# One fixed TensorE order for the attention of a transformer block: runs of eight transposes, the projection and the transposes of the residual moved

## The chip, the cores and the metric

The kernel runs on one core of one Trainium2 chip. The metric is device time in microseconds; lower is better. The core has a matrix engine (TensorE; PE in the profile, with PEld for its weight loads), a vector engine (VectorE, DVE), a scalar engine (ScalarE, ACT), GpSimd (POOL), and SyncE (SP), which here only issues DMA transfers. Each engine works through its own queue in order, and semaphores hold an instruction back until what it needs is there. TensorE writes its results into eight banks of PSUM, each 128 partitions by 512 floats; ACT and DVE read them from there.

## The reference

One block of 2048 tokens of width 1024 in float32: a normalised input goes through single-head attention with head width 256, its output is projected, normalised and added to the input, and the same is done with a gated feed-forward network (FFN) of hidden width 2752.

```python
def layernorm(x): return (x - mean(x)) / sqrt(var(x) + 1e-5)

def attention(x):                       # x: (1, 2048, 1024)
    q, k, v = split(x @ Wqkv + bqkv)    # each (2048, 256)
    a = softmax(q @ k.T / 16)           # (2048, 2048)
    return (a @ v) @ Wo + bo            # (2048, 1024)

def ffn(x):
    return (silu(x @ W_gate.T) * (x @ W_up.T)) @ W_down.T   # hidden width 2752

x = x + layernorm(attention(layernorm(x)))
x = x + layernorm(ffn(layernorm(x)))
```

## The kernel before

**Precision.** Almost every product is made of three matmuls of a fast 32-bit type. A matrix is split into a high part (`split`, L109: a cast on ACT) and a low part (L110: the source minus the high part, on DVE). `mm3` (L144 to L148) multiplies high by high, high by low and low by high into one PSUM bank.

**Stages.** From 0 to about 163 us the input is normalised and transposed, and q, k and v are made (`v_block`, L206 to L211, leaves its sum in bank 6 or 7, from which DVE takes it at L210 and L211). From about 163 to 437 us runs the attention with the projection and the first part of the residual. From then to the end the FFN runs as a Strassen-like scheme of products (L605).

**Attention.** The 2048 queries are 16 blocks (`NT`) of 128; the main loop (L898 to L940) goes over them, and in block i the following is called:

- `q_load` (L240), in blocks 4 and 8 (`TB` is 4): SP loads the next 512 queries, and ACT and DVE split them into `qa` or `qb`, the two buffers used in turn.
- `turn(i, j)` for j = 0 to 3 (L263 to L270): four 128x128 transposes of the exponentials `p_s` (L268) into bank 4 or 7, split into `pT` by ACT and DVE.
- `scores(i+1, j)` (L243 to L251): six 512-wide matmuls into bank j, and on DVE the row maximum of the bank (L251).
- `softmax(i+1)` (L253 to L261): DVE takes the maximum of four (L256) and multiplies it by -1/16 (L257); ACT makes four exponentials, each with its row sum (L259); DVE adds the sums and takes the reciprocal (L260, L261).
- a load of the rows of x into `pair[i % 3][1]`, for the residual, in the first 8 blocks (`EARLY`).
- `turn_o(i-1)` (L282 to L286): two transposes of the attention's output into bank 5 (L285), split into `oTs`.
- `attend(i)` (L272 to L280): for each of 16 blocks of keys a 512-wide (L276) and a 256-wide matmul (L277) into bank 6; ACT copies one half of the result (L279) and DVE adds the other (L280).
- `proj(i-1)` (L288 to L297): 12 matmuls with the output weights, six into bank 5 and six into bank 7; after each six DVE scales and adds the bias (L295). The weights `wo_s` share their memory (`wvo`) with the value weights of `v_block`.
- `xpose(i-2)`, in blocks 2 to 9 (L342 to L352): eight transposes (L347) of the normalised rows, four to a bank, into banks 6 and 5; ACT copies each bank out (L349) and SP stores it as FFN input (L351).
- `residual(i-1)`, in blocks 1 to 8 (L299 to L308): statistics on DVE (L116 twice, L119, L120), the power -1/2 on POOL (L121) and the product for the bias (L302), the normalisation on ACT (L303), the sum with x on DVE (L304) and its store (L305), statistics again with POOL (L307), and the second normalisation on ACT (L308), whose result `xpose` reads one block later in the loop.

In blocks 10 to 15 the first loads, sums and splits of the FFN are also called, and `feed` and `order` bring its first weights.

**What sets the order.** The lines above are only the order in which instructions are handed to the scheduler of the tile framework (`schedule_with_timeline_sim=True`). It puts the instructions of every engine into an order of its own, by its own timeline, as long as dependences through tiles and banks hold. `tc.keep_in_program_order` takes an instruction out of its choice: such instructions follow each other in the order of the program. Before, it is used in the FFN (under the name `pin`, L403) and for the late residuals' statistics. A long run of one kind therefore need not stay together: in this trace TensorE's attention is a mixture, such as one attend matmul between four transposes and a score matmul.

Of the kernel before, what the change touches and what calls it, by code (L numbers as in the profile page):

```python
# [11 lines left out]
ALU = mybir.AluOpType  # L12
# [3 lines left out]
P = 128  # L16
T = 2048
C = 1024
D = 256
F = 2752  # L20
NT = T // P
# [3 lines left out]
TB = G // P  # L25
FB = F // P
FR = F - FB * P
NKB = T // P
# [6 lines left out]
def block_kernel(ctx, tc, x, wqk, wv, bqk, bv, wo, bo, wgu, wlast, wd, out):  # L35
# [12 lines left out]
    nc = tc.nc  # L48
# [4 lines left out]
    def tl(p, shape, dt, name):  # L53
        return p.tile(shape, dt, tag=name, name=name, bufs=1)
# [3 lines left out]
    ident = tl(cpool, [P, P], F32, "ident")  # L58
# [18 lines left out]
    bank = [tl(bank_pool, [P, 512], F32, f"bank{i}") for i in range(8)]  # L77
# [27 lines left out]
    def f32(ap):  # L105
        return ap.bitcast(F32)

    def split(hi, lo, src, lo_engine=None):
        nc.scalar.copy(hi, src)  # L109
        (lo_engine or nc.vector).tensor_tensor(lo, src, f32(hi), ALU.subtract)  # L110
# [30 lines left out]
            cols = slice(tb * P, (tb + 1) * P)  # L141
            split(dst[:, 4 * hf : 4 * hf + 4, 0, cols], dst[:, 4 * hf : 4 * hf + 4, 1, cols], src)

    def mm3(o, w, m, first, last):  # L144

        nc.tensor.matmul(o, w[0], m[0], start=first, stop=False)  # L146
        nc.tensor.matmul(o, w[0], m[1], start=False, stop=False)  # L147
        nc.tensor.matmul(o, w[1], m[0], start=False, stop=last)  # L148


    def kT(d, g):
        return slot(kx, 4 * d + g)

    vt = a1.rearrange("p a b c -> p (a b c)").rearrange("p (k h d) -> p k h d", h=2, d=D)
# [75 lines left out]
    nc.scalar.dma_start(bo_s, bo.partition_broadcast(P))  # L230


    qraw = f4[4].rearrange("p (d q) -> p d q", d=2)
    pair = [(f4[0], f4[1]), (f4[2], f4[3]), (f2p[0], f2p[1])]
    wo_s = wvo.rearrange("p a b c -> p (a b c)").rearrange("p (d h c) -> p d h c", d=2, h=2)
    pT = [a2[:, 4 * i : 4 * i + 4, :, :].rearrange("p a b c -> p (a b c)").rearrange("p (k h q) -> p k h q", h=2, q=P) for i in range(2)]
    o_s = [f2[4][:, 0:D], f2[4][:, D:]]
    EARLY = 2 * TB

    def q_load(g):  # L240
        nc.sync.dma_start(qraw, q_d[g])
        split(qs[g % 2][:, :, 0, :], qs[g % 2][:, :, 1, :], qraw)

    def scores(i, j):

        cols = slice((i % TB) * P, (i % TB + 1) * P)
        q = qs[(i // TB) % 2]
        for d in range(2):
            k = kT(d, j)
            mm3(bank[j], (q[:, d, 0, cols], q[:, d, 1, cols]), (k[:, 0, :], k[:, 1, :]), d == 0, d == 1)  # L250
        nc.vector.tensor_reduce(ys[i % 4][:, j : j + 1], bank[j], AX.X, ALU.max)  # L251

    def softmax(i):  # L253

        s = ys[i % 4]
        nc.vector.tensor_reduce(s[:, 4:5], s[:, 0:4], AX.X, ALU.max)  # L256
        nc.vector.tensor_scalar(s[:, 5:6], s[:, 4:5], -1.0 / 16.0, None, ALU.mult)  # L257
        for j in range(4):
            nc.scalar.activation(p_s[:, j * 512 : j * 512 + 512], bank[j], AF.Exp, bias=s[:, 5:6], scale=1.0 / 16.0, accum_out=s[:, 8 + j : 9 + j])  # L259
        nc.vector.tensor_reduce(s[:, 12:13], s[:, 8:12], AX.X, ALU.add)  # L260
        nc.vector.reciprocal(s[:, 13:14], s[:, 12:13])  # L261

    def turn(i, j):  # L263

        b = bank[(4, 7)[j % 2]]
        for n in range(4):
            k = 4 * j + n
            nc.tensor.transpose(b[:, n * P : (n + 1) * P], p_s[:, k * P : (k + 1) * P], ident)  # L268
        d = pT[i % 2][:, 4 * j : 4 * j + 4, :, :]
        split(d[:, :, 0, :], d[:, :, 1, :], b.rearrange("p (n q) -> p n q", n=4))  # L270

    def attend(i):  # L272
        b = bank[6]
        p = pT[i % 2]
        for k in range(NKB):
            nc.tensor.matmul(b, p[:, k, 0, :], vt[:, k, :, :].rearrange("p h d -> p (h d)"), start=(k == 0), stop=False)  # L276
            nc.tensor.matmul(b[:, D:], p[:, k, 1, :], vt[:, k, 0, :], start=False, stop=(k == NKB - 1))  # L277
        o = o_s[i % 2]
        nc.scalar.copy(o, b[:, :D])  # L279
        nc.vector.tensor_tensor(o, b[:, D:], o, ALU.add)  # L280

    def turn_o(i):  # L282
        b = bank[5][:, 0:D]
        for d in range(2):
            nc.tensor.transpose(b[:, d * P : (d + 1) * P], o_s[i % 2][:, d * P : (d + 1) * P], ident)  # L285
        split(oTs[i % 2][:, :, 0, :], oTs[i % 2][:, :, 1, :], b.rearrange("p (d q) -> p d q", d=2))  # L286

    def proj(i):  # L288
        a = pair[i % 3][0] if i < EARLY else f4[i % 2]
        oT = oTs[i % 2]  # L290
        for h, b in ((1, bank[5]), (0, bank[7])):
            cols = slice(h * 512, h * 512 + 512)
            for d in range(2):
                mm3(b, (oT[:, d, 0, :], oT[:, d, 1, :]), (wo_s[:, d, 0, cols], wo_s[:, d, 1, cols]), d == 0, d == 1)
            nc.vector.scalar_tensor_tensor(a[:, cols], b, ys[i % 4][:, 13:14], bo_s[:, cols], ALU.mult, ALU.add)  # L295
        if i >= EARLY:
            nc.sync.dma_start(at_d[i], a)  # L297
# [26 lines left out]
    p_s = tl(spool, [P, T], F32, "p_s")  # L324
# [6 lines left out]
    for j in range(4):  # L331
        scores(0, j)
# [6 lines left out]
        split(wo_s[:, d, 0, :], wo_s[:, d, 1, :], f4[d])  # L339


    def xpose(t, a, b, banks):  # L342
        for hf in range(2):
            o = banks[hf]
            for j in range(4):
                cb = 4 * hf + j
                nc.tensor.transpose(o[:, j * P : (j + 1) * P], a[:, cb * P : (cb + 1) * P], ident)  # L347
            s = b[:, hf * 512 : hf * 512 + 512]
            nc.scalar.copy(s, o)  # L349
            d = xT_d[t // TB][hf * 512 : hf * 512 + 512, (t % TB) * P : (t % TB + 1) * P]  # L350
            nc.sync.dma_start(d.rearrange("(j p) t -> p j t", p=P), s.rearrange("p (j t) -> p j t", j=4))  # L351
# [28 lines left out]
    L, R = slice(0, 512), slice(512, 1024)  # L380
# [19 lines left out]

    pin = tc.keep_in_program_order  # L403

    def split_later(dst, src):

        pin(nc.scalar.copy(dst[:, :, 0, :], src))
        pin(nc.vector.tensor_tensor(dst[:, :, 1, :], src, f32(dst[:, :, 0, :]), ALU.subtract))

    def first_load(cb, r1, r2):  # L410
        load_xq(r1, 0, cb)
        load_xq(r2, 1, cb)

    def first_sums(cb, r1, r2):
        split_later(by_half(xb)[:, :, cb], two(r1))
        sum_x(r1, r2)
        nc.sync.dma_start(xs_d[cb][0], r1)
        nc.sync.dma_start(xs_d[cb][1], r2)

    class First:  # L420
# [10 lines left out]
        def use(self):  # L431
            split_later(self.dst, two(self.r))
# [43 lines left out]
    class Slot:  # L476
        t = None
# [139 lines left out]
    def add(o, a, b, op=ALU.add):  # L617
        nc.vector.tensor_tensor(o, a, b, op)  # L618
# [122 lines left out]
    def down_weights(p):  # L741

        r1, r2 = f4[0:2]
        pin(nc.vector.tensor_tensor(r2[:, R], r2[:, R], r1[:, R], ALU.subtract))
        add(r1[:, R], r1[:, R], r1[:, L], ALU.subtract)
        add(r1[:, L], r2[:, R], r1[:, L])
        add(r2[:, L], r2[:, L], r1[:, L], ALU.subtract)
        for n, t in (("T1", r1[:, R]), ("T3", r2[:, R]), ("T2", r1[:, L]), ("T4", r2[:, L])):
            nc.sync.dma_start(td[p][n], t)
# [148 lines left out]
    room = [(f4[2], f4[3]), (wr[1], xe)]  # L898
    for i in range(NT):
        more = i + 1 < NT  # L900
        if i % TB == 0 and TB <= i < NT - TB:
            q_load(i // TB + 1)
        turn(i, 0)
        turn(i, 1)
        if more:
            scores(i + 1, 0)
            scores(i + 1, 1)
        turn(i, 2)
        turn(i, 3)
        if more:  # L910
            scores(i + 1, 2)
            scores(i + 1, 3)
            softmax(i + 1)
        if i < EARLY:
            nc.sync.dma_start(pair[i % 3][1], x[i * P : (i + 1) * P, :])
        if i > 0:
            turn_o(i - 1)
        if i == NT - 1:
            for f in order[:4]:
                f.use()  # L920
        attend(i)
        if i > 0:
            proj(i - 1)
        if 2 <= i < EARLY + 2:
            xpose(i - 2, *pair[(i - 2) % 3], (bank[6], bank[5]))
        if 0 < i <= EARLY:
            residual(i - 1, *pair[(i - 1) % 3])
        cb = i - EARLY - 3
        if 0 <= cb < 4:
            first_sums(cb, *room[cb % 2])  # L930
        if 0 <= cb + 1 < 4:
            first_load(cb + 1, *room[(cb + 1) % 2])
        if i == NT - 4:
            feed.pump()
        if i == NT - 2:
            for n in range(2):
                slots.free(flat(a2[:, 2 * n : 2 * n + 2, :, :]))
            feed.pump()
            order = [t2[0], t13[0], t13[1], t13[2], t2[1], t13[3]] + t4
            spare = f4[2], f4[3], wr[1], xe  # L940
            for f, r in zip(order, spare):
                f.load(r)
    turn_o(NT - 1)
    proj(NT - 1)

    last = f4[2], f4[3], wr[1], bo_s
# [103 lines left out]
```

## Time and profile before

| What | Value |
|---|---|
| median of 3 runs | 1701.09 us (1698.03 to 1702.44) |
| the profiled execution's own time | 1700.9 us |
| span of the profile | 1699.1 us, 21099 instructions |
| TensorE clock granted in 40 slices | nine tenths or more in every slice |
| transfers over the span | 271.00 MB, mean 159 GB/s |

The span reaches from the first to the last instruction that the profiler saw; the remaining 1.8 us lie around it. The profile divides the span into 40 slices of 42.5 us. Its digits are tenths of the slice in which the engine was busy, and 9 means 90% or more:

```profile
PE   8999999999899999999999999999999999999997
DVE  8643667667787777776578457866555665455458
ACT  3222445544544444443365444433333333344343
```

Slices 5 to 10 are the attention; in slice 11 the FFN begins, and TensorE's digit falls to 8 there. The costliest groups of instructions are all matmuls of the FFN (columns: line, engine, operation, output and inputs, shape, number; busy us and mean ns of one; idle us of the engine just before them):

```profile
L605 PE MATMUL bank<-a 128*128 128x512 f32 x1164 | 274.2, 389 | 0.0
...
L605 PE MATMUL bank<-xb,a 128*128 128x512 f32 x912 | 212.3, 389 | 0.1
...
L276 PE MATMUL bank<-a,a 128*128 128x512 f32 x256 | 94.6, 403 | 2.8 <-ACT f L349 2.0
```

A group's mean is the length of the record of one instruction; consecutive matmuls overlap, so the records of one engine add up to more than its busy time. The last column of the third line names who ended most of the idle time in front of the attend matmuls.

### The profile page before, as it was taken

How to read it: one execution, taken by the hardware profiler on the slowest of the kernel's cores; microseconds unless marked ns; L12 is line 12 of the kernel's file. 1: busy time of each engine (PE TensorE's matmuls, PEld its weight loads, DVE VectorE, ACT ScalarE, POOL GpSimd, SP SyncE). 2: the span in 40 equal slices, each digit the busy share in tenths (PEclk: the TensorE clock that was granted, in tenths of full speed). 3: DMA queues.
4: the chain of work that ended last, by engine and by line, in shares of the span. 5: the costliest groups of instructions: out<-in, count | busy, mean ns of one | idle time of the engine just before them, and what ended most of it. 6: DMA issues, size and time to landing. Idle time of an engine off the chain costs nothing.

```text
span 1699.1 us, 21099 instructions
## 1 busy us (share of the span) xinstructions
PE 1669.2 (98%) x7764; PEld 1385.5 (82%) x7764; DVE 1100.3 (65%) x1682; ACT 694.8 (41%) x1039; POOL 91.3 (5%) x118
## 2 busy tenths in 40 slices
PE   8999999999899999999999999999999999999997
PEld 6888887888678888888888888788888888888886
DVE  8643667667787777776578457866555665455458
ACT  3222445544544444443365444433333333344343
POOL 1000000000011211110000000100000000000001
PEclk9999999999999999999999999999999999999999
DMA  6221123334676566665367666633332223566654
GB/s 214 81 81 38 38 75 121 101 118 169 218 243 209 200 215 212 217 220 183 122 204 252 215 191 198 210 106 113 130 111 100 93 94 124 209 221 192 195 189 158
DMA packets 131014, 271.00 MB, mean 159 GB/s; under 512 B 13280, under 2 KB 29792, under 8 KB 130912
## 3 DMA queue, kind: packets, MB, share of 16 engines
q1 hardware_dynamic: 128176, 262.72, 46.5%
q10 hardware_dynamic: 2736, 6.95, 1.2%
q8 instruction: 60, 0.98, 0.2%
q14 instruction: 42, 0.34, 0.1%
HBM read 185.73 MB, written 83.89 MB: 159 GB/s over the span
## 4 chain that ended last, share of the span: by engine, by line
PE 92%; DVE 4%; DMA 2%; ACT 1%; issue 1%; POOL 0%; SPq 0%; POOLq 0%; DVEq 0%; ACTq 0%
PE bank L605 69%; PE bank L146 4%; PE bank L147 4%; PE bank L148 4%; PE bank L276 3%; PE bank L277 2%; PE bank L206 2%; PE bank L268 1%; PE bank L207 1%; PE bank L347 1%; PE bank L139 1%; DVE a L110 1%; DVE small L116 0%; DMA f<-xT_d 0%; DVE wvo L110 0%
## 5 line engine op out<-in xcount | busy, mean ns | idle before, releaser
L605 PE MATMUL bank<-a 128*128 128x512 f32 x1164 | 274.2, 389 | 0.0
L605 PEld LDWEIGHTS bank<-a 128*128 128x128 f32 x1164 | 218.5, 188 | 45.3
L605 PE MATMUL bank<-xb,a 128*128 128x512 f32 x912 | 212.3, 389 | 0.1
L605 PEld LDWEIGHTS bank<-xb,a 128*128 128x128 f32 x912 | 171.1, 188 | 36.0 <-ACT xi L621 0.6
L618 DVE TENSOR_TENSOR xi<-bank,xi 128x512 f32<-128x512 f32 (+1 forms) x170 | 114.0, 682 | 115.0 <-PE bank L605 70.1
L110 DVE TENSOR_TENSOR a<-f2p,a 128x1024 fp32r<-128x1024 f32 (+2 forms) x133 | 134.6, 1012 | 58.0 <-ACT a L109 54.0
L109 ACT CAST a<-f2p 128x1024 fp32r<-128x1024 f32 (+2 forms) x133 | 117.5, 884 | 131.7 <-PE bank L605 107.2
L110 DVE TENSOR_TENSOR a<-f,a 128x1024 fp32r<-128x1024 f32 (+2 forms) x91 | 89.9, 988 | 106.5 <-ACT a L109 99.8
L605 PE MATMUL bank<-wvo 128*128 128x512 f32 x612 | 149.6, 389 | 0.0
L605 PE MATMUL bank<-kx,a 128*128 128x512 f32 x612 | 146.2, 389 | 0.0
L605 PE MATMUL bank<-a,a 128*128 128x512 f32 x588 | 140.2, 390 | 3.8 <-ACT xi L661 2.6
L605 PEld LDWEIGHTS bank<-kx,a 128*128 128x128 f32 x612 | 114.9, 188 | 23.8
L605 PEld LDWEIGHTS bank<-wvo 128*128 128x128 f32 x612 | 114.9, 188 | 23.9
L605 PEld LDWEIGHTS bank<-a,a 128*128 128x128 f32 x588 | 110.2, 188 | 27.5 <-ACT xi L661 3.0
L109 ACT CAST a<-f 128x1024 fp32r<-128x1024 f32 (+2 forms) x91 | 69.5, 764 | 141.6 <-PE bank L605 110.3
L605 PE MATMUL bank<-a,wvo 128*128 128x512 f32 x444 | 106.3, 389 | 0.0
L605 PE MATMUL bank<-kx,wvo 128*128 128x512 f32 x420 | 100.1, 389 | 0.0
L605 PEld LDWEIGHTS bank<-a,wvo 128*128 128x128 f32 x444 | 83.3, 188 | 17.3
L276 PE MATMUL bank<-a,a 128*128 128x512 f32 x256 | 94.6, 403 | 2.8 <-ACT f L349 2.0
L110 DVE TENSOR_TENSOR wvo<-f,wvo 128x1024 fp32r<-128x1024 f32 (+1 forms) x52 | 60.8, 1169 | 54.9 <-ACT wvo L109 53.8
L605 PEld LDWEIGHTS bank<-kx,wvo 128*128 128x128 f32 x420 | 78.8, 188 | 16.4
L618 DVE TENSOR_TENSOR xi<-xi,xi 128x512 f32<-128x512 f32 (+1 forms) x124 | 85.3, 688 | 5.6 <-ACT xi L621 1.5
(233 smaller groups left out, 2677.5 us busy)
## 6 DMA issues: line engine op xcount, KB each, us to landing
f2p<-wgu SPq DMA_DIRECT2D x41, 512.0 KB, 5.6
hd_S<-xi SPq DMA_DIRECT2D x80, 256.0 KB, 4.4
f<-x SPq DMA_DIRECT2D x30, 512.0 KB, 3.8
hd_A<-xi SPq DMA_DIRECT2D x60, 256.0 KB, 2.0
f<-wgu SPq DMA_DIRECT2D x22, 512.0 KB, 3.5
wr<-wgu SPq DMA_DIRECT2D x21, 512.0 KB, 5.9
f<-wd SPq DMA_DIRECT2D x20, 512.0 KB, 5.0
td_T<-f SPq DMA_DIRECT2D x40, 256.0 KB, 4.6
```

The lines of the kernel that those rows point to most:

```text
L109: nc.scalar.copy(hi, src)
L110: (lo_engine or nc.vector).tensor_tensor(lo, src, f32(hi), ALU.subtract)
L139: nc.tensor.transpose(b[:, j * P : (j + 1) * P], t[:, cb * P : (cb + 1) * P], ident)
L146: nc.tensor.matmul(o, w[0], m[0], start=first, stop=False)
L147: nc.tensor.matmul(o, w[0], m[1], start=False, stop=False)
L148: nc.tensor.matmul(o, w[1], m[0], start=False, stop=last)
L206: nc.tensor.matmul(b, xg[:, c, 0, cols], wv_s[:, c, :, :].rearrange("p a f -> p (a f)"), start=(c == 0), stop=False)
L207: nc.tensor.matmul(b[:, D:], xg[:, c, 1, cols], wv_s[:, c, 0, :], start=False, stop=(c == 7))
L276: nc.tensor.matmul(b, p[:, k, 0, :], vt[:, k, :, :].rearrange("p h d -> p (h d)"), start=(k == 0), stop=False)
L277: nc.tensor.matmul(b[:, D:], p[:, k, 1, :], vt[:, k, 0, :], start=False, stop=(k == NKB - 1))
L605: one = nc.tensor.matmul(o, w[i], m[j], start=first and n == 0, stop=last and n == 2, skip_group_check=chained)
L618: nc.vector.tensor_tensor(o, a, b, op)
```

## The change

It does four things.

1. A new `pin` hands every TensorE instruction of the attention to `keep_in_program_order` in blocks 0 to 12 (`ORDERED` is `NT - 3`, and `block[0]` holds the block that the loop is in). It covers `scores` (not those of block 0 in front of the loop), `turn`, `attend`, `turn_o`, `proj` and, through an argument, `xpose`. The matmuls of the last three blocks stay with the scheduler. The name `pin` of the FFN becomes `keep`.
2. In the program's order, `turn_o(i-1)` stands directly behind `turn(i, 2)` and `turn(i, 3)`, and `xpose(i-2)` directly behind `attend(i)`, ahead of `proj(i-1)`.
3. The banks: the second half of `proj` goes to bank 6, where it went to bank 7; `xpose` goes to banks 4 and 7, where it went to 6 and 5.
4. `q_load` is called in blocks 5 and 9 behind the softmax, where it was called at the start of blocks 4 and 8.

Lines behind the new helper lie further down in the changed kernel: L303 becomes L311, L308 becomes L316, L347 becomes L355.

```diff
--- before.py
+++ after.py
@@ -141,11 +141,11 @@
             cols = slice(tb * P, (tb + 1) * P)
             split(dst[:, 4 * hf : 4 * hf + 4, 0, cols], dst[:, 4 * hf : 4 * hf + 4, 1, cols], src)
 
-    def mm3(o, w, m, first, last):
-
-        nc.tensor.matmul(o, w[0], m[0], start=first, stop=False)
-        nc.tensor.matmul(o, w[0], m[1], start=False, stop=False)
-        nc.tensor.matmul(o, w[1], m[0], start=False, stop=last)
+    def mm3(o, w, m, first, last, pin=lambda i: i):
+
+        pin(nc.tensor.matmul(o, w[0], m[0], start=first, stop=False))
+        pin(nc.tensor.matmul(o, w[0], m[1], start=False, stop=False))
+        pin(nc.tensor.matmul(o, w[1], m[0], start=False, stop=last))
 
 
     def kT(d, g):
@@ -230,6 +230,14 @@
     nc.scalar.dma_start(bo_s, bo.partition_broadcast(P))
 
 
+
+    ORDERED = NT - 3
+    block = [0]
+
+    def pin(i):
+        return tc.keep_in_program_order(i) if block[0] < ORDERED else i
+
+    free = lambda i: i
     qraw = f4[4].rearrange("p (d q) -> p d q", d=2)
     pair = [(f4[0], f4[1]), (f4[2], f4[3]), (f2p[0], f2p[1])]
     wo_s = wvo.rearrange("p a b c -> p (a b c)").rearrange("p (d h c) -> p d h c", d=2, h=2)
@@ -247,7 +255,7 @@
         q = qs[(i // TB) % 2]
         for d in range(2):
             k = kT(d, j)
-            mm3(bank[j], (q[:, d, 0, cols], q[:, d, 1, cols]), (k[:, 0, :], k[:, 1, :]), d == 0, d == 1)
+            mm3(bank[j], (q[:, d, 0, cols], q[:, d, 1, cols]), (k[:, 0, :], k[:, 1, :]), d == 0, d == 1, pin if i else free)
         nc.vector.tensor_reduce(ys[i % 4][:, j : j + 1], bank[j], AX.X, ALU.max)
 
     def softmax(i):
@@ -265,7 +273,7 @@
         b = bank[(4, 7)[j % 2]]
         for n in range(4):
             k = 4 * j + n
-            nc.tensor.transpose(b[:, n * P : (n + 1) * P], p_s[:, k * P : (k + 1) * P], ident)
+            pin(nc.tensor.transpose(b[:, n * P : (n + 1) * P], p_s[:, k * P : (k + 1) * P], ident))
         d = pT[i % 2][:, 4 * j : 4 * j + 4, :, :]
         split(d[:, :, 0, :], d[:, :, 1, :], b.rearrange("p (n q) -> p n q", n=4))
 
@@ -273,8 +281,8 @@
         b = bank[6]
         p = pT[i % 2]
         for k in range(NKB):
-            nc.tensor.matmul(b, p[:, k, 0, :], vt[:, k, :, :].rearrange("p h d -> p (h d)"), start=(k == 0), stop=False)
-            nc.tensor.matmul(b[:, D:], p[:, k, 1, :], vt[:, k, 0, :], start=False, stop=(k == NKB - 1))
+            pin(nc.tensor.matmul(b, p[:, k, 0, :], vt[:, k, :, :].rearrange("p h d -> p (h d)"), start=(k == 0), stop=False))
+            pin(nc.tensor.matmul(b[:, D:], p[:, k, 1, :], vt[:, k, 0, :], start=False, stop=(k == NKB - 1)))
         o = o_s[i % 2]
         nc.scalar.copy(o, b[:, :D])
         nc.vector.tensor_tensor(o, b[:, D:], o, ALU.add)
@@ -282,16 +290,16 @@
     def turn_o(i):
         b = bank[5][:, 0:D]
         for d in range(2):
-            nc.tensor.transpose(b[:, d * P : (d + 1) * P], o_s[i % 2][:, d * P : (d + 1) * P], ident)
+            pin(nc.tensor.transpose(b[:, d * P : (d + 1) * P], o_s[i % 2][:, d * P : (d + 1) * P], ident))
         split(oTs[i % 2][:, :, 0, :], oTs[i % 2][:, :, 1, :], b.rearrange("p (d q) -> p d q", d=2))
 
     def proj(i):
         a = pair[i % 3][0] if i < EARLY else f4[i % 2]
         oT = oTs[i % 2]
-        for h, b in ((1, bank[5]), (0, bank[7])):
+        for h, b in ((1, bank[5]), (0, bank[6])):
             cols = slice(h * 512, h * 512 + 512)
             for d in range(2):
-                mm3(b, (oT[:, d, 0, :], oT[:, d, 1, :]), (wo_s[:, d, 0, cols], wo_s[:, d, 1, cols]), d == 0, d == 1)
+                mm3(b, (oT[:, d, 0, :], oT[:, d, 1, :]), (wo_s[:, d, 0, cols], wo_s[:, d, 1, cols]), d == 0, d == 1, pin)
             nc.vector.scalar_tensor_tensor(a[:, cols], b, ys[i % 4][:, 13:14], bo_s[:, cols], ALU.mult, ALU.add)
         if i >= EARLY:
             nc.sync.dma_start(at_d[i], a)
@@ -339,12 +347,12 @@
         split(wo_s[:, d, 0, :], wo_s[:, d, 1, :], f4[d])
 
 
-    def xpose(t, a, b, banks):
+    def xpose(t, a, b, banks, pin=lambda i: i):
         for hf in range(2):
             o = banks[hf]
             for j in range(4):
                 cb = 4 * hf + j
-                nc.tensor.transpose(o[:, j * P : (j + 1) * P], a[:, cb * P : (cb + 1) * P], ident)
+                pin(nc.tensor.transpose(o[:, j * P : (j + 1) * P], a[:, cb * P : (cb + 1) * P], ident))
             s = b[:, hf * 512 : hf * 512 + 512]
             nc.scalar.copy(s, o)
             d = xT_d[t // TB][hf * 512 : hf * 512 + 512, (t % TB) * P : (t % TB + 1) * P]
@@ -400,12 +408,12 @@
 
 
 
-    pin = tc.keep_in_program_order
+    keep = tc.keep_in_program_order
 
     def split_later(dst, src):
 
-        pin(nc.scalar.copy(dst[:, :, 0, :], src))
-        pin(nc.vector.tensor_tensor(dst[:, :, 1, :], src, f32(dst[:, :, 0, :]), ALU.subtract))
+        keep(nc.scalar.copy(dst[:, :, 0, :], src))
+        keep(nc.vector.tensor_tensor(dst[:, :, 1, :], src, f32(dst[:, :, 0, :]), ALU.subtract))
 
     def first_load(cb, r1, r2):
         load_xq(r1, 0, cb)
@@ -741,7 +749,7 @@
     def down_weights(p):
 
         r1, r2 = f4[0:2]
-        pin(nc.vector.tensor_tensor(r2[:, R], r2[:, R], r1[:, R], ALU.subtract))
+        keep(nc.vector.tensor_tensor(r2[:, R], r2[:, R], r1[:, R], ALU.subtract))
         add(r1[:, R], r1[:, R], r1[:, L], ALU.subtract)
         add(r1[:, L], r2[:, R], r1[:, L])
         add(r2[:, L], r2[:, L], r1[:, L], ALU.subtract)
@@ -898,8 +906,7 @@
     room = [(f4[2], f4[3]), (wr[1], xe)]
     for i in range(NT):
         more = i + 1 < NT
-        if i % TB == 0 and TB <= i < NT - TB:
-            q_load(i // TB + 1)
+        block[0] = i
         turn(i, 0)
         turn(i, 1)
         if more:
@@ -907,22 +914,24 @@
             scores(i + 1, 1)
         turn(i, 2)
         turn(i, 3)
+        if i > 0:
+            turn_o(i - 1)
         if more:
             scores(i + 1, 2)
             scores(i + 1, 3)
             softmax(i + 1)
+        if i % TB == 1 and TB < i < NT - TB:
+            q_load(i // TB + 1)
         if i < EARLY:
             nc.sync.dma_start(pair[i % 3][1], x[i * P : (i + 1) * P, :])
-        if i > 0:
-            turn_o(i - 1)
         if i == NT - 1:
             for f in order[:4]:
                 f.use()
         attend(i)
+        if 2 <= i < EARLY + 2:
+            xpose(i - 2, *pair[(i - 2) % 3], (bank[4], bank[7]), pin)
         if i > 0:
             proj(i - 1)
-        if 2 <= i < EARLY + 2:
-            xpose(i - 2, *pair[(i - 2) % 3], (bank[6], bank[5]))
         if 0 < i <= EARLY:
             residual(i - 1, *pair[(i - 1) % 3])
         cb = i - EARLY - 3
```

## Prediction

> **What bounds the kernel now.** I read the page's header and the shares by engine of its chain of waits first, then the busy time by stage, then the list of what TensorE waited for.
>
> ```profile
> PE 1669.2 (98%) x7764; PEld 1385.5 (82%) x7764; DVE 1100.3 (65%) x1682; ACT 694.8 (41%) x1039; POOL 91.3 (5%) x118
> ...
> PE 92%; DVE 4%; DMA 2%; ACT 1%; issue 1%; POOL 0%; SPq 0%; POOLq 0%; DVEq 0%; ACTq 0%
> ```
>
> TensorE is busy 98% of the span and is 92% of the chain: only its own instruction time and its pauses count. The stages follow; columns are busy us (and instructions) of PE, PEld, DVE, ACT, POOL, then granted clock, DMA share and GB/s.
>
> ```profile
> 163.00:300.00 137.00, 133.08 (x732) 111.54 (x731) 90.94 (x187) 66.79 (x137) 9.80 (x24) 1.00 0.23 74
> 300.00:437.00 137.00, 136.93 (x746) 116.01 (x745) 93.97 (x174) 63.43 (x130) 3.26 (x8) 1.00 0.40 138
> 437.00:500.00 63.00, 54.54 (x239) 43.30 (x238) 50.44 (x72) 31.74 (x44) 6.07 (x5) 1.00 0.69 229
> 500.00:1680.00 1180.00, 1178.67 (x5226) 975.77 (x5225) 761.75 (x1040) 487.30 (x649) 57.10 (x55) 1.00 0.53 175
> ```
>
> The changed stage, 163 to 437 us, leaves TensorE idle 3.92 + 0.07 = 4.0 us. A matmul's record lasts 0.39 us although the next starts 0.23 later, so a pause shows about 0.16 too short; over some eleven pauses that is 1.7. Measured from start to start the stage loses **5.7 us**: a fixed order can save no more by removing waits. Some are in the list of waits (total us, times, longest); the L637 waits lie behind the attention:
>
> ```profile
> PE bank L605 <- ACT xi L637: 3.1, 2, 1.6
> ...
> PE bank L276 <- ACT f L349: 2.0, 2, 1.4
> ...
> PE bank L276 <- ACT a L109: 0.7, 1, 0.7
> ```
>
> **What the Trainium skill says.** "Perfetto Trace Analysis", Tensor Engine Instruction: TensorE's end times are computed from size, and ACT and DVE run strictly in queue order. The trace agrees: in the timeline below the attend (L276) waits 1.43 us for a copy (L349, 276.63) that stood behind the first normalisation (L303, 275.49). "TensorE: Matmul & The Clock Gate", Part 2, Step-by-step: only weight loads are pulled ahead, matmuls stay in program order. So a waiting pinned transpose stops everything behind it; no run here contradicts it. "PSUM — Partial Sum Buffer", Terms: two engines must not be on one bank at once; the banks' handoffs count, as at L211 below.
>
> ```profile
> 275.49 1.24 ACT L303 ACTIVATE f<-f,small 128x1024 f32<-128x1024 f32 x1
> ...
> 276.63 0.56 ACT L349 COPY f<-bank 128x512 f32<-128x512 f32 x1
> ...
> 277.25 0.50 PE L276 MATMUL bank<-a,a 128*128 128x512 f32 x1 [1.43 <-ACT f L349]
> ...
> 277.84 0.71 ACT L259 ACTIVATE p_s<-bank,ys 128x512 f32<-128x512 f32 x1
> ...
> 278.51 0.71 ACT L259 ACTIVATE p_s<-bank,ys 128x512 f32<-128x512 f32 x1
> ```
>
> **The change, part by part.** The changed kernel's built order has, for i = 0 to 12, exactly: turn 0 and 1, scores(i+1, 0 and 1), turn 2 and 3 with turn_o(i−1), scores(i+1, 2 and 3), attend(i), for i = 2 to 9 xpose(i−2), proj(i−1). Blocks 13 to 15 stay mixed with the first products of the FFN. No TensorE work is added or removed, so only pauses and switches count.
>
> Units, as pitches from start to start in the attention's timeline: 512-wide matmul 0.231, 256-wide 0.117, transpose 0.109 (four in 0.44, eight in 0.87); exp with its accumulator read 0.67 (277.84 to 278.51); ACT copy of 512 columns 0.48, of 1024 1.145 (record 1.25); DVE 512 columns 0.60 (record 0.68), 1024 columns 1.14, 256 columns 0.33. From a last matmul's start its consumer starts 0.43 later, from a transpose's 0.31; back to TensorE costs 0.055.
>
> *Pauses removed:* the fixed order takes away the causes above, −5.7; what comes in their place is counted below.
>
> *Longer runs of transposes:* per transpose they save nothing (0.87 for 8). At the switches the 81 runs of before lose 6.2 us against these pitches, of which 855 matmuls × 4 ns = 3.4 are a drift of the matmuls; 2.8/81 × 33 runs fewer = 1.1, and if all were switches 2.5. Between 0 and −2.5 I take −1.4.
>
> *xpose behind attend.* This is the main term. xpose(i−2) reads the second normalisation (L308, L316 after) of residual(i−2), which runs in the same block i. ACT's built order there is the four casts of the turns, L303, oTs cast, the four exps of block i+1, **then** L308, then the o copy. Count from turn 0's start. TensorE: turns 0.87, scores 12 × 0.231 to 3.65, turns and turn_o to 4.74, scores to 7.51, attend 16 × (0.231 + 0.117) = 5.57, so xpose could start at 13.09. ACT finishes the turns' casts near 5.25 and L303 at 6.5. DVE meanwhile does lo2, lo3 and one max, 4.98 to 6.9; then x + a (L304) to 8.05, oTs lo to 8.4, the max of bank 3 to 9.08, two BN statistics to 10.3, the small max and −1/16 to 10.58. Exps 10.6 + 4 × 0.67 = 13.28; L308 ends 14.52; xpose starts 14.58. Stall 14.58 − 13.09 = **1.49**, in 8 blocks **11.9**. Behind the xpose wait proj(i−1) and every later block; the POOL chain for L308 (1.03 us after the eps, near 11.9) is hidden by the exps. If DVE had no backlog the stall would be about 1.0, 8.0 in all. These rows give the durations:
>
> ```profile
> L259 ACT ACTIVATE p_s<-bank,ys 128x512 f32<-128x512 f32 x60 | 41.1, 697 | 5.0 <-DVE ys L257 5.0
> L303 ACT ACTIVATE f<-f,small 128x1024 f32<-128x1024 f32 x6 | 7.5, 1248 | 0.0
> L308 ACT ACTIVATE f<-f,small 128x1024 f32<-128x1024 f32 x6 | 7.5, 1244 | 4.4 <-POOL small L307 4.4
> L116 DVE BATCH_NORM_STATS2 small<-f 128x6 f32<-128x512 f32 x24 | 16.0, 685 | 0.2
> ```
>
> *q_load moved* to blocks 5 and 9: DVE's split of qa/qb (1024 columns, 1.14) stands in blocks 2 and 6 ahead of the max that releases the exps: 2 × 1.14 = +2.3 (none if DVE has slack there). Its load from SP is hidden: SP's queue is not in the chain and the DMA share is 0.23 here.
>
> *proj's second half in bank 6*, which attend just used: in blocks 2 to 9 the o add (ready about 15.3) is covered by stall and xpose, 14.58 + 0.87 = 15.45, plus proj's first half of 1.4. Elsewhere the first half itself covers the 1.2 us from attend's last matmul to the add. Cost 0; bound +0.3 × 5 if that cover were gone.
>
> *Block 0.* Turn 1 now needs bank 7 with nothing between. That bank holds the last v_block's result, whose evacuation stands in DVE's order behind the splits of wo:
>
> ```profile
> 171.09 0.42 DVE L210 TENSOR_TENSOR f<-bank,bv_s 128x256 f32<-128x256 f32 x1
> ...
> 171.43 1.21 DVE L110 TENSOR_TENSOR wvo<-f,wvo 128x1024 fp32r<-128x1024 f32 x1
> ...
> 172.56 0.42 DVE L211 TENSOR_TENSOR f<-bank,f 128x256 f32<-128x256 f32 x1
> ```
>
> On before TensorE filled this with scores. In the built order of after, turn 0's lo split (0.60) also stands ahead of L211: free at 172.56 + 0.60 + 0.43 + 0.055 = 173.64 on this clock. The last v matmul starts at 170.34, so turn 1 is ready at 170.34 + 0.117 + 0.44 = 170.90: **2.75**. If these splits did not stand ahead, about 1. The clock gate page ("What's actually happening") puts the idle window that may lower the clock at 3.4 us: no pause here reaches it, and before shows a clock of 1.00 throughout.
>
> *Tail, 437 to 500.* Idle before is 63 − 54.54 = 8.46, 8.9 from start to start. After, the order of the last blocks is of the same kind; one ACT copy of the first FFN products stands behind a cast that waits for a load (I take 3.2, between 0.7 and 6). With the other pauses (0.6 + 0.9 + 1.8 + 2.6) it is 9.1: +0.2, bounds −2.3 and +3.
>
> **Sum.** Against the profiled execution (1700.9; span 1699.1 plus 1.8 around it): 1700.9 − 5.7 − 1.4 + 11.9 + 2.3 + 2.75 + 0.2 = 1710.95, so **1711.0**; the median of the runs is 0.2 from that execution.
>
> **Rivals.**
> - *A, forecast* (chance 0.61): xpose waits as counted, 1711.0, own range 1707 to 1715.
> - *B, the same wait, but small* (0.14): DVE has no backlog (8.0 for 11.9, no +2.3) and block 0 loses only 1: 1711.0 − 3.9 − 2.3 − 1.75 = 1703.0 to 1706. For: DVE is busy only 90.94 of 137 us. Against: BN, max and splits follow each other at once in before (0.2 us idle ahead of 24 BN statistics).
> - *C, not slower* (0.15): L308 is done before attend ends. It decides from exps that start by 13.09 − 0.055 − 1.25 − 2.68 = 9.1 in the block in place of 10.6, or from an L308 ahead of the exps. Then the 11.9 and 2.3 go: 1711.0 − 14.2 = 1696.8. For: before spends 15.4 us of DVE waiting for scores, so DVE may run ahead. Against: the built ACT order and the 6.9 at which the wide add starts.
> - *D, the tail loses more* (0.10): the cast behind the load takes 6 us and the FFN starts late: +3, with 1 to 2 for pauses behind it, 1715 to 1717. For: DMA share 0.69 there. Against: the loads are issued blocks ahead.
> - That the change doesn't do what it says is excluded for blocks 0 to 12 by the built order.
>
> **Range and chances.** 0.3% of 1701.1, about what can be told from no change, is 5.1 us: faster below 1696.0, slower above 1706.2. A lies almost wholly above it, D above it, B at or below it, C around the faster edge. So faster 0.07, within 0.3% 0.18, slower 0.75. The range reaches from B's lower part to D: 1702 to 1717; C and the ends are left out.
>
> **What would show it.** The waits list of after should carry "PE bank (the xpose line) <- ACT f (second normalisation)" about 8 times at some 1.5 us, 12 to 14 in all; one wait of about 2.8 us of the turns for DVE's L211; no attend wait on an xpose copy. PE idle in the stretch 163 to about 330 should rise to some 15 to 17 us, and blocks 2 to 9 last 16.7 + 1.5 = 18.2 us. L308 with no wait, or exps starting by 9.1 us in the block, would prove A wrong and C right; FFN pauses of over 12 us in all would prove D.

## The result, and the profile after

| | median of 5 runs | lowest to highest |
|---|---|---|
| before | 1700.23 us | 1698.03 to 1702.44 |
| after | 1717.38 us | 1714.87 to 1719.05 |

The changed kernel is slower: the ratio of its runs to those of before is 1.0098, 95% interval 1.0084 to 1.0113. The profiled execution took 1715.3 us (span 1713.1), so 14.4 of the 17.2 us are in the traces that are compared here.

The stages, in the busy times by stretch (columns as before: PE, PEld, DVE, ACT, POOL, granted clock, DMA share, GB/s), of the changed kernel:

```profile
163.00:300.00 137.00, 125.86 (x691) 106.70 (x690) 85.31 (x175) 61.81 (x127) 8.87 (x22) 0.99 0.22 74
300.00:437.00 137.00, 132.65 (x718) 111.90 (x717) 87.46 (x171) 59.63 (x130) 4.14 (x11) 1.00 0.33 114
437.00:500.00 63.00, 56.81 (x246) 45.98 (x245) 51.02 (x70) 32.29 (x45) 6.49 (x3) 0.92 0.70 225
500.00:1680.00 1180.00, 1177.49 (x5227) 975.32 (x5226) 758.59 (x1026) 486.44 (x649) 55.77 (x52) 1.00 0.54 177
```

Two things are to be seen. TensorE's idle time in the two attention stretches rose from 4.0 to 11.14 + 4.35 = 15.5 us. And the granted clock, 1.00 in the third stretch before, is 0.92 there now. The list of what TensorE waited for (total us, times, longest) names the pauses of the changed kernel:

```profile
PE bank L355 <- ACT f L316: 12.4, 7, 2.5
PE bank L146 <- DVE kx L416: 3.5, 1, 3.5
PE bank L276 <- DVE f L211: 2.7, 1, 2.7
PE bank L355 <- ACT f2p L316: 2.5, 2, 1.3
```

L355 is xpose and L316 the second normalisation: nine waits, of which eight lie in blocks 2 to 9 and one, of 2.5 us, in the FFN. L276 behind L211 is turn 1 of block 0. L146 behind L416 is the last projection, and this one was not in the prediction. The attend's waits on an xpose copy (2.0) are gone from the list.

The timeline of block 4, whose turn 0 starts at 238.01, shows how a wait of xpose comes about (start us, duration us, engine, line, operation; in brackets the idle time before and who ended it):

```profile
247.02 1.27 DVE L116 BATCH_NORM_STATS2 small<-f2p 128x6 f32<-128x512 f32 x2
248.46 0.10 DVE L265 TENSOR_SCALAR ys<-ys 128x1 f32<-128x1 f32 x1
...
248.60 0.69 ACT L267 ACTIVATE p_s<-bank,ys 128x512 f32<-128x512 f32 x1 [3.83 <-DVE ys L265]
250.60 0.69 ACT L267 ACTIVATE p_s<-bank,ys 128x512 f32<-128x512 f32 x1
251.26 1.25 ACT L316 ACTIVATE f2p<-f2p,small 128x1024 f32<-128x1024 f32 x1
...
252.56 1.09 PE L355 MATMUL bank<-ident,f2p 128*128 128x128 f32 x8 [1.24 <-ACT f2p L316]
```

DVE's two statistics stand ahead of the −1/16 (248.46), so the exps start 10.59 us into the block, L316 waits behind all four of them although ACT had been idle for 3.83 us before, and xpose starts at 14.55. The brackets say 1.24 because they count from the modelled end of the last attend matmul; from start to start it is 1.40 more than without a wait.

### The profile page after: what moved, and what is told of

It is laid out like the page before. It is cut to its first block, busy times and chain, and to the rows that moved or that the text cites. A ratio compares the mean times of both kernels' runs of the same rounds, so it can differ in the third digit from the quotient of the medians.

```text
span 1713.1 us, 21075 instructions
## 1 busy us (share of the span) xinstructions
PE 1673.3 (98%) x7764; PEld 1390.5 (81%) x7764; DVE 1099.7 (64%) x1682; ACT 692.5 (40%) x1039; POOL 93.9 (5%) x118
## 4 chain that ended last, share of the span: by engine, by line
PE 79%; DVE 2%; ACT 1%; issue 1%; DMA 1%; POOL 0%; DVEq 0%; POOLq 0%; SPq 0%; ACTq 0%
PE bank L613 71%; PE bank L146 1%; PE bank L148 1%; PE bank L147 1%; PE bank L284 1%; PE bank L276 1%; PE bank L355 1%; ACT p_s L267 1%; PE bank L285 1%; PE bank L792 0%; PE bank L793 0%; DVE small L116 0%; ACT f L316 0%; DMA xT_d<-f 0%; DVE wvo L110 0%
## 5 line engine op out<-in xcount | busy, mean ns | idle before, releaser
L613 PE MATMUL bank<-a,a 128*128 128x512 f32 x588 | 139.9, 389 | 0.0
L284 PE MATMUL bank<-a,a 128*128 128x512 f32 x256 | 91.1, 398 | 0.0
```

The costliest lines, as they stand in the source:

```text
L284: pin(nc.tensor.matmul(b, p[:, k, 0, :], vt[:, k, :, :].rearrange("p h d -> p (h d)"), start=(k == 0), stop=False))
L613: one = nc.tensor.matmul(o, w[i], m[j], start=first and n == 0, stop=last and n == 2, skip_group_check=chained)
```

## The experiments

Thirteen traces are compared below in two numbers, both from 163 to 520 us: *pauses* is my own sum of the time from one TensorE start to the next above the usual pitch, wherever that excess is over 0.4 us; *half clock* is the number of stretches of 3.4 us in which the trace shows a granted clock of 0.50. Such a stretch costs up to 1.7 us. A late pause near 520 can fall inside or outside, so the sums are good to a microsecond or two.

| kernel | median us | ratio to before, 95% interval | pauses, us | half clock |
|---|---|---|---|---|
| before | 1700.2 | | 14.4 | 0 |
| after | 1717.4 | 1.0098 [1.0084, 1.0113] | 26.8 | 4 |
| e1 no pins | 1706.0 | 1.0040 [1.0025, 1.0055] | 15.0 | 2 |
| e2 xpose behind proj | 1720.3 | 1.0121 [1.0104, 1.0138] | 25.0 | 7 |
| e3 the same, old banks | 1704.1 | 1.0027 [1.0019, 1.0034] | 16.0 | 2 |
| e4 q_load back | 1719.0 | 1.0112 [1.0097, 1.0127] | 29.0 | 5 |
| e5 proj's bank back | 1716.5 | 1.0112 [1.0097, 1.0127] | 29.4 | 1 |
| e6 no pins, proj's bank back | 1702.8 | 1.0026 [1.0017, 1.0035] | 13.2 | 0 |
| e7 pins from block 1 | 1717.3 | 1.0108 [1.0093, 1.0123] | 26.3 | 5 |
| e8 repaired | 1697.1 | 0.9993 [0.9985, 1.0002] | 11.8 | 0 |
| e9 bank 7 in the tail only | 1714.1 | 1.0090 [1.0076, 1.0104] | 26.6 | 1 |
| e10 e8 with xpose first | 1711.1 | 1.0075 [1.0059, 1.0091] | 23.4 | 2 |
| e11 e8 with a split on POOL | 1697.5 | 0.9991 [0.9983, 0.9999] | 9.9 | 1 |

The ratios of e1 to e11 are to runs of before beside them on the same chip, with medians of 1698.7 to 1699.8 us; the experiments ran on three chips, so small differences between them are better read in the ratios. A traced execution is one of a kernel's runs and not always a typical one: that of e5 took 4.2 us more than its median, of which some 3.4 lie ahead of the attention, and that of e10 3.8 us more.

**e1: no pins.** The rest of the change stays.

```diff
-        return tc.keep_in_program_order(i) if block[0] < ORDERED else i
+        return tc.keep_in_program_order(i) if block[0] < 0 else i
```

> The changed kernel with no instruction pinned: program order, banks and the moved calls stay. Theory A (the fixed order makes TensorE stand still for the second normalisation): the waits of xpose on L316 (12.4 us in blocks 2 to 9 of the changed kernel) and the 2.7 us of block 0 shrink to under 3 us in all, and the time falls by 12 to 17 us, to 1700 to 1705. Rival (the moved calls and banks cost it, with pins or without): at least 1710.

It took 1706.0 us, 11.4 less than the changed kernel but 6 more than before; the rival's 1710 is excluded, and the top of the forecast is missed by one. The waits list of e1:

```profile
PE bank L146 <- DVE kx L416: 3.8, 1, 3.8
...
PE bank L355 <- ACT f L316: 1.0, 1, 1.0
```

The wait of xpose is gone from the attention (the one left is in the FFN), that of block 0 too; the wait of the last projection is still there. So the pins make the first two, and something else in the change makes the last.

**e2: xpose behind proj,** all else as in the changed kernel.

```diff
-        if 2 <= i < EARLY + 2:
-            xpose(i - 2, *pair[(i - 2) % 3], (bank[4], bank[7]), pin)
         if i > 0:
             proj(i - 1)
+        if 2 <= i < EARLY + 2:
+            xpose(i - 2, *pair[(i - 2) % 3], (bank[4], bank[7]), pin)
```

> The changed kernel with xpose(i-2) behind proj(i-1), all else pinned as it is. Theory A: xpose is then due 2.8 us later than its data, its waits on L316 go (12.4 to under 1), but the second half of proj comes to bank 6 before the o copy behind L316 has freed it: a new wait of some 0.85 us in each of blocks 2 to 9, 2.0 in blocks 2 and 6, 9 in all. Net 5 to 7 us less than the changed kernel, 1710 to 1713. Rival (the data of xpose was not the limit, ACT or DVE is too slow for the block): the waits stay at 12 or more under another name, 1716 to 1719.

The time, 1720.3 us, missed the forecast and even the rival's band. The waits went as theory A says in kind: none of xpose in the attention, and instead

```profile
PE bank L146 <- DVE f L288: 6.1, 4, 2.0
```

proj's second half waits in bank 6 for the o add (L288), in four blocks (2, 4, 6 and 10) with 2.1 us in blocks 2 and 6, not in eight. In six blocks turn 0 also waits 0.45 us for the copy of xpose out of bank 4. The pauses fell by only 1.8 us, and seven stretches ran at half clock where the changed kernel had four; why there are more here is taken up at the end.

**e3: xpose behind proj with the banks of before.** The diff of e2, and:

```diff
-        for h, b in ((1, bank[5]), (0, bank[6])):
+        for h, b in ((1, bank[5]), (0, bank[7])):
...
+            xpose(i - 2, *pair[(i - 2) % 3], (bank[6], bank[5]), pin)
```

> As the run before, and with the banks of the kernel before (second half of proj in bank 7, xpose in banks 6 and 5). Theory A with the wait for bank 6: both waits go, blocks 2 to 9 last 16.7 us in place of 18.2 (20.9 and 19.4 in blocks 6 and 2), no half clock in the attention; 1699 to 1703. Rival (DVE or ACT is the limit of a block in this order): blocks of 17.5 us or more, over 1708.

1704.1 us, a microsecond above the forecast and far from the rival's. Blocks 3 to 5 and 7 to 9 last 16.8 us, blocks 2 and 6 18.9 and 18.2 (a wait of 1.4 of xpose on the o add behind the queries' split). The forecast of no half clock failed: block 0's pause of 2.8 us was followed by it. ACT and DVE therefore keep up with a fixed order; it was the place of xpose and the banks that stopped TensorE.

**e4: q_load back** at the start of blocks 4 and 8.

```diff
+        if i % TB == 0 and TB <= i < NT - TB:
+            q_load(i // TB + 1)
...
-        if i % TB == 1 and TB < i < NT - TB:
-            q_load(i // TB + 1)
```

> The changed kernel with q_load called at the start of blocks 4 and 8 again. Theory A: the splits of the next queries leave the way of the maxima in blocks 2 and 6 or come elsewhere with the same 1.14 us; if they leave, the waits in these two blocks fall from 2.5 to 1.4 us and the half clock after the longer one (1.5 us) goes: 2 to 4 us less, 1713.5 to 1715.5. Rival (their place makes no difference): 1716 to 1719.

The rival was right: 1719.0 us, and the waits of xpose in blocks 2 and 6 stay at 2.6 and 2.5 us. The split is not pinned, and the scheduler puts it into blocks 2 and 6 wherever it is called: DVE's part starts at 206.22 and 275.62 in before, at 210.56 and 284.66 in the changed kernel, at 212.04 and 286.13 here. That is when the old queries in its buffer have been read for the last time, five blocks ahead of need: the queries split in block 2 are first used at 296.21, in block 7. So the move of q_load costs nothing that can be seen; the early split in a pinned order does.

**e5: only proj's bank back** (the first two lines of e3's diff).

> The changed kernel with only the bank of proj's second half undone (bank 7 again). Theory T (bank 6, which the last attend also needs, puts the last blocks' work into the order that makes the last projection wait): the pause of 3.7 us ahead of the last proj shrinks below 1.5 and the half clock behind it goes, 1711 to 1715; the waits of xpose stay at 12 to 13 us in the attention. Rival (the other moved calls make it, above all turn_o): pause and time stay, 1716 to 1719.

1716.5 us: by the time alone the rival. But the pause ahead of the last proj fell from 3.6 to 0.6 us, with no wait on L416 left. It is paid for elsewhere: eleven waits of turn 1 for proj's result in bank 7 (L276 behind L303, 5.1 us in all, none in the changed kernel), since bank 7 is needed again 0.231 + 0.44 = 0.67 us after proj's last matmul starts. The time was no test of theory T here; the waits spoke for it.

**e6: no pins and proj's bank back** (both diffs).

> The run without pins (1706.0) with the bank of proj's second half undone too, so that only the moved calls of q_load, turn_o and xpose are left. Theory T: the tail's pause goes here too, 1699 to 1702, no different from the kernel before. Rival: 1705 to 1707.

1702.8 us, 3.2 less than e1, just above the forecast, and the wait on L416 is gone here too. With e1 this divides the change roughly: of the 17.2 us the pins hold 11.4 and proj's bank 3.2, which leaves 2.6 for the moved calls and xpose's banks. By the ratios, since the runs are from different chips, it is 0.58, 0.14 and 0.26% of the time: about 10, 2.4 and 4.4 us. Where the last part lies stays open: e6's trace has no half clock and no more pauses than before, and turn_o's move was not undone by itself.

**e7: pins from block 1.**

```diff
-        return tc.keep_in_program_order(i) if block[0] < ORDERED else i
+        return tc.keep_in_program_order(i) if 0 < block[0] < ORDERED else i
```

> The changed kernel with block 0 left to the scheduler, pins from block 1 to 12. Theory A: the wait of 2.7 us for the evacuation of bank 7 (L211) and the half clock that follows it in some runs (1.5 us) go, 1713 to 1715. Rival (the same DVE work only makes TensorE wait later in block 0 or 1): 1716 to 1719.

The wait of 2.7 us for L211 went; 0.8 and 0.5 us of smaller pauses came in its place, as in before. That leaves 1.5 us, and the trace has one more stretch at half clock, in block 2. In the median, 1717.3, nothing of it can be seen: inconclusive in time.

**e8: all repairs together.** Pins from block 1, xpose behind proj, and the banks so that each is free when it is next due:

```diff
-        for h, b in ((1, bank[5]), (0, bank[6])):
+        for h, b in ((1, bank[7]), (0, bank[5])) if i < ORDERED else ((1, bank[5]), (0, bank[7])):
...
+            xpose(i - 2, *pair[(i - 2) % 3], (bank[7], bank[6]), pin)
```

> All repairs together: pins from block 1 to 12, xpose behind proj and in banks 7 and 6, proj in banks 7 and 5 in the pinned blocks (bank 7 is then free 1.4 us earlier for the next turn) and in 5 and 7 in the last three. Theory A: pinned blocks without stalls, 15.9 us (16.7 with xpose), apart from 1.4 us in blocks 2 and 6 behind the splits of the next queries; 1697 to 1701, at or just below the kernel before. Rival (a fixed order of DVE and ACT work stalls elsewhere in the block): over 1703.

1697.1 us. Blocks last 15.9 us, 16.75 to 16.85 with xpose, and 17.8 to 17.9 in blocks 2 and 6; no stretch at half clock is left. Against before it is 0.9993, with 1 in the interval: the repairs take back all that the change cost, and a gain over before is not shown.

**e9: bank 7 in the last four projections only.** Blocks 0 to 12 as in the changed kernel.

```diff
-        for h, b in ((1, bank[5]), (0, bank[6])):
+        for h, b in ((1, bank[5]), (0, bank[6] if i < ORDERED - 1 else bank[7])):
```

> The changed kernel with bank 7 for proj's second half in the last four calls only (proj 12 to 15); blocks 0 to 12 as they were. Theory T: the pause of 3.4 to 4.0 us ahead of the last proj falls to about 0.7, with 1.5 to 2.1 ahead of the last turn_o, and no half clock behind it; the waits of xpose stay. 1711.5 to 1714.5, 3 to 6 less than the changed kernel. Rival (the tail's pause comes from something else than this bank, or another takes its place): 1716 to 1719.

1714.1 us, 3.3 less, within the forecast. By the ratios (1.0090 against 1.0098) it is 1.4 us less, with intervals that overlap, so the gain in time is not sure. In the trace it is plain what happened: the pause ahead of the last proj is 0.6, that ahead of the last turn_o 1.6, and no half clock follows. With e5 and e6, where the wait on L416 went too, this shows that the bank made this pause. The sum of the pauses hardly fell (26.6 against 26.8 us), because one of 1.6 ahead of the last turn_o and 1.3 more in block 10 came in; what the trace gained is three stretches less at half clock. How a bank comes to this is in the two timelines. The changed kernel:

```profile
443.73 0.68 DVE L392 TENSOR_TENSOR wr<-wr 128x512 f32<-128x512 f32 x1
...
444.68 0.42 SPq L425 DMA_DIRECT2D xs_d<-wr  x1
449.61 0.80 SPq L437 DMA_DIRECT2D wr<-xs_d  x2
...
453.39 1.04 ACT L415 CAST kx<-wr 128x1024 fp32r<-128x1024 f32 x1 [3.15 <-DMA wr<-xs_d]
454.34 1.04 ACT L415 CAST kx<-xe 128x1024 fp32r<-128x1024 f32 x1
455.29 0.36 ACT L109 CAST oTs<-bank 128x256 fp32r<-128x256 f32 x1
...
455.71 0.79 PE L146 MATMUL bank<-wvo,oTs 128*128 128x512 f32 x1 [3.48 <-DVE kx L416]
```

and e9:

```profile
438.22 0.69 DVE L392 TENSOR_TENSOR wr<-wr 128x512 f32<-128x512 f32 x1
...
438.93 0.32 SPq L425 DMA_DIRECT2D xs_d<-wr  x1
...
445.79 1.05 ACT L415 CAST kx<-wr 128x1024 fp32r<-128x1024 f32 x1 [3.14 <-DMA wr<-xs_d]
...
455.16 0.37 ACT L109 CAST oTs<-bank 128x256 fp32r<-128x256 f32 x1 [1.32 <-PE bank L293]
```

The FFN's sums (L392) are stored and their buffer is loaded again before ACT can cast it (L415). With bank 6 the scheduler's order on DVE has these sums 5.5 us later, at 443.73, and the last oTs cast stands in ACT's queue behind the two casts, which wait for the load. With bank 7 the casts are done 7 us before the oTs cast is due. The name in the brackets, DVE kx L416, is only the event that came last; the projection waits for ACT's oTs.

**e10: the repaired kernel with xpose first** again, in banks 4 and 6.

```diff
+        if 2 <= i < EARLY + 2:
+            xpose(i - 2, *pair[(i - 2) % 3], (bank[4], bank[6]), pin)
         if i > 0:
             proj(i - 1)
-        if 2 <= i < EARLY + 2:
-            xpose(i - 2, *pair[(i - 2) % 3], (bank[7], bank[6]), pin)
```

> The repaired kernel (1697.1) with one thing put back: xpose(i-2) between attend(i) and proj(i-1), in banks 4 and 6. Theory A: waits of some 1.4 us in blocks 2 to 9 and 2.5 in blocks 2 and 6 come back, 12 to 14 us in all, and 0 to 3 for half clock: 1709 to 1714. Rival (the wait of xpose costs only in company with the other parts of the change): under 1704.

1711.1 us, 14.1 more than e8, and its waits list has them again:

```profile
PE bank L355 <- ACT f L316: 9.7, 6, 2.4
...
PE bank L355 <- ACT f2p L316: 2.3, 2, 1.3
```

The trace has 11.6 us more of pauses and two stretches at half clock. One of its banks moved with xpose, from 7 to 4, but the waits are for the second normalisation and not for a bank. So the place of xpose carries the main term without the other parts of the change.

**e11: the repaired kernel with the queries' low part on POOL.**

```diff
-        split(qs[g % 2][:, :, 0, :], qs[g % 2][:, :, 1, :], qraw)
+        split(qs[g % 2][:, :, 0, :], qs[g % 2][:, :, 1, :], qraw, nc.gpsimd)
```

> The repaired kernel with the low part of the next queries' split on POOL in place of DVE. Theory A: the pauses of 1.0 us in blocks 2 and 6 go, 1.5 to 2 us: 1695 to 1697. Rival (POOL's power for the normalisation then waits behind the split): the same or up to 3 us more, 1697 to 1700.

The two pauses of 1.0 us in blocks 2 and 6 are gone from the trace, as theory A says, but a pause of 2.1 us ahead of the last turn_o brought half clock (1.6 us) in this trace. 1697.5 us is no better than e8. The interval of 0.9991 ends at 0.9999, just clear of 1; among eleven kernels compared that is a faint lead, if it is one.

## Why the prediction came out as it did

It was right in direction, and in the cause and place of the main loss. The size was too small: forecast were 1711.0 us with 1702 to 1717, measured 1717.4, just past the upper end, which reached that far only for rival D. The traced execution is 4.3 us above the forecast. Half clock, put at nothing, cost 5.3 us there (TensorE's small excesses over its usual pitch inside the four stretches); the other terms together are about 1 us below the forecast. Step by step:

- *Pauses removed, −5.7.* Nearly right: before had six pauses over 0.4 us in its attention, 5.0 us in all, and none of them is left.
- *Longer runs of transposes, −1.4.* It fits. At the FFN's 60th matmul the changed kernel is 19.4 us later. Its pauses up to there are 15.3 us longer (24.0 against 8.7) and half clock cost it 5.3 us, 20.6 in all; the 1.2 us between are saved in small steps. That they are saved at the switches was not shown separately.
- *xpose behind attend, 1.49 in eight blocks and 2.3 in two of them, 14.2 in all.* Right: 1.40 to 1.47 in six blocks, 2.57 and 2.51 in blocks 2 and 6, together 13.7. The exps start at 10.59 in the block (10.6 forecast), xpose at 14.55 (14.58). TensorE's idle time to 330 us is 13.8, under the 15 to 17 named as a sign: the eighth wait comes at 345 us, and idle time in the records leaves out 0.16 us of each pause. e10 shows it without the rest of the change. Only the heading was wrong: the 2.3 belong to the queries' split, which stood in blocks 2 and 6 before as well, not to the move of q_load (e4).
- *Block 0, 2.75.* Right, 2.83, and for the reason given: in the changed kernel's timeline

```profile
170.79 0.68 DVE L110 TENSOR_TENSOR a<-bank,a 128x512 fp32r<-128x512 f32 x1
171.40 0.41 DVE L211 TENSOR_TENSOR f<-bank,f 128x256 f32<-128x256 f32 x1
...
171.95 0.63 PE L276 MATMUL bank<-ident,p_s 128*128 128x128 f32 x4 [2.67 <-DVE f L211]
```

turn 0's low split stands ahead of L211, and turn 1 behind it.

- *proj's second half in bank 6, cost 0.* Right in blocks 0 to 12 of the changed kernel but for one pause of 0.59 us in block 10; in blocks 2 to 9 stall and xpose cover the o add, and e2 shows its price without that cover (6.1 us). Wrong in the tail, where the bank changed the scheduler's order.
- *Tail, +0.2 with bounds −2.3 and +3.* Met in its sum by luck, and wrong in its content. From 437 to 520 us the pauses are 9.6 us against 9.4 before. But the forecast put the ACT copy of the first FFN products behind a cast that waits for a load; it was the last oTs cast that stood behind such a cast, and the pause cost 3.6 us. Over the last attention work the pauses are 6.9 us against 3.7 before, and the clock took some 3.5 more. The FFN then gave 5 us back: the lag of 19.4 us at its 60th matmul is 14.3 at its last, with one pause of 2.7 in place of the 2.8, 1.8 and 1.2 that before has between 460 and 500, and none in place of 1.3 at 1103.
- *The clock: "no pause here reaches it".* **This is the step that failed:** lost clock was put at nothing, and it took 5.3 us. The 3.4 us were taken there as a bound for one pause. In the changed kernel's windows the pause of 2.5 us in block 6 is followed by half clock (the column ahead of the DMA share):

```profile
283.80:287.20 3.40, 3.40 (x21) 2.92 (x20) 2.44 (x7) 1.04 (x3) 0.71 (x2) 1.00 0.36 129
287.20:290.60 3.40, 1.05 (x8) 0.73 (x7) 0.56 (x3) 3.13 (x8) 0.10 (x1) 0.99 0.37 140
290.60:294.00 3.40, 3.40 (x12) 2.91 (x11) 0.19 (x1) 1.17 (x2) 0.00 (x0) 0.51 0.44 124
294.00:297.40 3.40, 3.40 (x20) 2.89 (x19) 3.09 (x5) 1.07 (x2) 0.00 (x0) 1.00 0.51 155
```

The third stretch did 12 instructions where its neighbours did 20: 1.6 us lost. The traced execution has four such stretches between 163 and 520 us, the one of before none. The runs' granted clocks fit: 0.993 for the span of 1712.7, 0.992 for 1713.1 and 0.991 for those of 1715.2 to 1716.9 us, and 0.001 of 1713 us is 1.7 us, one such stretch. That some runs had more of them than the profiled one would explain the 2.1 us by which the median lies above it; those runs were not traced, so this stays argued.

Of the rivals, A held. The time came out at the end of D's band (1715 to 1717, A and a longer tail together), and a cast behind the load did stop TensorE there. But D's own sign, over 12 us of FFN pauses, did not come: they are 9.6 us. D was near in time, but it put the tail's loss down to pauses, and it was the clock's.

## What to carry to other kernels

A fixed order turns every late input into a pause of everything behind it, so each pinned instruction needs its producer's place in its own engine's queue checked, with all that stands ahead of it there; here moving one consumer 2.8 us later, and giving it banks that are free by then, was worth 14 us. A change of buffer can cost most in a stage where it was not made for its own sake, because the scheduler then orders other engines' work anew; look at the last blocks and the seams between stages separately. And where pauses of over 2 us are forecast, add time at the lower clock to their price, as worked out below.

## What was not expected of the hardware

A pause of 2 to 3 us sometimes lowers TensorE's clock and sometimes does not. Over the thirteen traces, counted between 100 and 1680 us from one TensorE start to the next, all 7 pauses of over 3.3 us were followed by half clock, and 14 of the 28 pauses of 2.2 to 3.0 us. The same pause of 2.94 us in block 0 (2.84 above the usual pitch) was followed by it in three of six traces.

The traces show what decides. In each of them all changes of the granted clock lie on one grid of steps of 3.413 us, to within 0.003 us. I divided each trace from 20 to 1680 us into these steps and summed, for each step, the time that TensorE lost above its usual pitch at full clock. Of the 6268 steps at full clock 24 were followed by a step at half clock: in these TensorE had lost 2.08 to 3.28 us. In all others it had lost 2.02 us or less. The limit thus lies near 2.05 of 3.41 us lost in one step, in one pause or in several. Whether a second step at half clock follows agrees with the same limit: 7 of 31 such steps were followed by another, with 2.05 us or more lost in them, the others with at most 1.88.

So it matters how a pause falls on the grid. In the changed kernel the pause of 2.51 us in block 6, shown above, ends 0.4 us ahead of a change of step and lies wholly in one step; half clock follows. That of 2.57 us in block 2 is divided, 1.90 and 0.67 us, and the clock stays at 1.00:

```profile
212.00:215.41 3.41, 1.67 (x10) 1.21 (x8) 0.46 (x4) 3.29 (x9) 0.81 (x2) 1.00 0.46 154
215.41:218.83 3.42, 2.75 (x16) 2.44 (x17) 0.65 (x2) 1.95 (x4) 0.00 (x0) 1.00 0.14 35
```

The grid starts at another offset in each trace, so for one pause this is chance. An estimate from these figures: a lone pause of 2.5 us puts 2.05 us or more into one step in (2.5 + 3.41 − 2 × 2.05) / 3.41 = 0.53 of its positions, which is about the 14 of 28 seen; at up to 1.7 us for each step, its price is 0.9 us on top of the pause. For the pauses of 2.75, 2.6 and 2.6 us that the prediction itself forecast this gives 3 us.

This agrees in part with what the Trainium skill says of the clock ("TensorE: Matmul & The Clock Gate", What's actually happening): its window of about 3.4 us runs freely and is not reset when a kernel starts. That at least one idle window must pass before the clock drops does not hold here: no step was idle from end to end, and 2.08 us lost were enough. The limit was found in traces that were already there; no run was made to test it. It gives the reason why e2, whose trace has six pauses of over 2 us, came out slower than its sum of waits.
